# Emptying a convolution's PSUM on ScalarE instead of VectorE, with q placed between two pairs of spread attention weights

## The chip, the cores and the metric

The kernel runs on one core of one Trainium2 chip. A core has five engines that run their own instruction streams side by side: TensorE (PE: matmuls and transposes, its weight loads shown as PEld), VectorE (DVE), ScalarE (ACT), GpSimd (POOL) and SyncE (SP, which here only issues transfers). The metric is the device time in microseconds (us); it was 5517.69 us, the median of three runs (5511.05 to 5520.15).

## What is computed

Eight images of 256 channels and 64 x 64 pixels pass through two layers in fp32. Layer 0 adds a local attention over 3 x 3 neighbourhoods, with a second set of weights that a small generator makes from q, k and v. Layer 1 adds a deformable 3 x 3 convolution: for each pixel and each of nine taps an offset and a mask are computed, four neighbouring pixels are gathered, mixed, and multiplied with the convolution's weights.

```python
def _L0_conv_ref(x, ...):
    qkv = einsum('oc,bchw->bohw', w_qkv, x)              # q, k, v; 4 heads of 64 channels
    logits = einsum('bhdl,bhdkl->bhkl', q_flat, k_patch) # k: the 9 neighbours
    attn_out = einsum('bhkl,bhdkl->bhdl', softmax(logits, axis=2), v_patch)
    kernel = einsum('hkc,bhcl->bhkl', w_kg_g, cat) + b_kg
    conv_out = einsum('bhkl,bhdkl->bhdl', kernel, v_patch)
    return einsum('oc,bchw->bohw', w_proj, alpha * conv_out + beta * attn_out)

def _L1_conv_ref(x, w_off, b_off, w):                    # deformable convolution
    om = conv3x3(x, w_off) + b_off                       # 9 x (dy, dx), 9 masks
    v = the bilinear mix of the 4 pixels around each of the 9 moved taps, times sigmoid(mask)
    return einsum('bckhw,ock->bohw', v, w)

x = x + _L0_conv_ref(_gn(x), ...)                        # _gn: group norm, 32 groups
x = x + _L1_conv_ref(_gn(x), ...)                        # the x added here is called x1 below
```

## The kernel before

An image is cut into NC = 8 chunks of eight rows, N = 512 pixels. For layer 1 a chunk has KK = 9 taps, and a chunk with one tap is a slot: 72 slots an image, 576 in all. A slot's 512 pixels are NB = 4 blocks of 128, so there are 2304 blocks.

The main loop (the last lines of `preact_kernel`) walks the slots. In slot n, `transposes` turns the four summed blocks s on PE into PSUM (tile pt) and ACT copies them to SBUF (tile vt); `product(n - 1)` then multiplies the vt of the slot before with the weights into po, the two PSUM banks of pool `ps_o` in which the nine taps of a chunk add up: eight matmul instructions of 128 x 512, L848. `ahead(i)` works in advance for later slots and is called twice in each: two blocks' first corner is scaled by ACT (`scale`, L802), the other three corners of two earlier blocks are added by DVE (`sum_corners`, L810, six instructions), and POOL issues two gathers (`gather`, L786), each of 128 rows of 4 KB from the table in DRAM. Ten gathered blocks g have buffers, and ten sums s.

After nine taps a chunk ends. `finished` (L859) adds po and x1, which was read back from DRAM into r at the fifth tap, on DVE, and r is stored. Until both adds are done the next chunk's first `product` can't write po. In such a slot (the variable `last`) both calls of `ahead` stand before `product` and `finished`.

All else for the next image is cut into steps, a generator (`fronts`), of which about one runs in each slot, behind the product: 64 steps of attention (eight chunks of eight steps), some for the ends and norms, then `prepare`, which writes the next table and finds the offsets, one chunk a step. The first image's steps all run before the first slot, and beside the last image's slots there are none.

In attention, chunk c's steps also hold the second half of chunk c - 1 (d in the code). The first step of a chunk runs `d.spread_weights()`: four matmuls (tile wk, L492), each from 9 partitions of its own group of 32, spread the weights of a head over 100 keys, and DVE masks each from PSUM to SBUF (L500). Then `q` makes two tiles of q (psq, L293), which ACT copies (L301). The last chunk's weights are spread in a step of their own. All these results pass through `psum_a`, a pool of four PSUM banks used in turn: a new tile waits until the tile four before it has been read. Ahead of wk stand one bank for w and two for vk, which ACT copies.

`second_stats` stores each finished chunk of x1 to DRAM (`kept`, L565), from where `product` reads it back into r; `image`, the copy in SBUF, is overwritten by the next image during `prepare`. `to_table` (L648 to L657) turns a chunk, copies it into ts, one of four row buffers, and SP stores each twice in the table.

The order of instructions on PE, ACT, DVE and POOL is that of the program text (`tc.manual_schedule`); SP's order is left to the scheduler. Each engine works its own queue in order, so an instruction that waits holds up all behind it.

Of the kernel before, what the change touches and what calls it, by code (L numbers as in the profile page):

```python
# [9 lines left out]
F32 = mybir.dt.float32  # L10
# [7 lines left out]
P = 128  # L18
C = 256
NT = C // P  # L20
# [4 lines left out]
N = R * W  # L25
NB = N // P
NC = H // R
KK = 9
HEADS = 4
# [6 lines left out]
TP = R * WP // TJ  # L36
T = 8
KT = T + 2
# [8 lines left out]
SLOTS = NC * KK  # L47
# [10 lines left out]
def preact_kernel(ctx: ExitStack, tc: tile.TileContext, a: dict, out: bass.AP):  # L58
# [123 lines left out]
    p1 = ctx.enter_context(tc.tile_pool(name="p1", bufs=1))  # L182
    p2 = ctx.enter_context(tc.tile_pool(name="p2", bufs=2))

    wp = ctx.enter_context(tc.tile_pool(name="wp", bufs=NC + 3))
    ps_a = ctx.enter_context(tc.tile_pool(name="ps_a", bufs=4, space=PSUM))
    ps_t = ctx.enter_context(tc.tile_pool(name="ps_t", bufs=2, space=PSUM))
    ps_o = ctx.enter_context(tc.tile_pool(name="ps_o", bufs=1, space=PSUM))
# [90 lines left out]
    class Attention:  # L279
# [97 lines left out]
        def logits(self):  # L377

            G = self.G
            qk = self.qk.rearrange("p j c h (y x) -> p (j c h y) x", x=KT)  # L380
            by = p1.tile([P, G * KT, 3], F32, tag="by", name=f"by_{self.u}")
            nc.vector.tensor_reduce(
                by, qk[:, :, 0:9].rearrange("p g (a x) -> p g x a", x=3), AX.X, ALU.add
            )
            nc.vector.tensor_add(by[:, :, 0], by[:, :, 0], qk[:, :, 9])
            by = by.rearrange("p (g y) x -> p g (y x)", y=KT)
            self.lt = lt = p1.tile([P, G, KK], F32, tag="lt", name=f"lt_{self.u}")
            nc.vector.tensor_reduce(
                lt, by[:, :, 0:27].rearrange("p g (a k) -> p g k a", k=KK), AX.X, ALU.add
            )  # L390
            nc.vector.tensor_add(lt[:, :, 0:3], lt[:, :, 0:3], by[:, :, 27:30])
# [84 lines left out]
        def weights(self):  # L476
            ps = psum_a(f"w_{self.u}")
            for j in range(NB):
                nc.tensor.transpose(
                    ps[:, j * P : (j + 1) * P],  # L480
                    wts2[self.c % 2][:, j].rearrange("p h k -> p (h k)"),
                    ident,
                )
            self.wsb = p1.tile([P, N], F32, tag="wsb", name=f"wsb_{self.u}")
            nc.scalar.copy(self.wsb, ps)

        def spread_weights(self):

            self.wk = []
            for h in range(HEADS):  # L490
                ps = psum_a(f"wk_{self.u}_{h}")
                nc.tensor.matmul(  # L492
                    ps[:NK],
                    spread[32 * h : 32 * h + KK],
                    self.wsb[32 * h : 32 * h + KK],
                    start=True,
                    stop=True,
                )
                wk = p2.tile([NK, N], F32, tag="wk", name=f"wk_{self.u}_{h}", bufs=HEADS)
                nc.vector.tensor_mul(  # L500
                    wk.rearrange("p (t n) -> p t n", n=T * T),
                    ps[:NK].rearrange("p (t n) -> p t n", n=T * T),
                    near.unsqueeze(1).to_broadcast([NK, TC, T * T]),
                )
                self.wk.append(wk)
# [18 lines left out]
        def weighted(self, i):  # L524
            n = N // NH
            if i == 0:
                self.acc = p1.tile([P, NT, N], F32, tag="acc", name=f"acc_{self.u}")
            av = psum_a(f"av_{self.u}_{i}").rearrange("p (m n) -> p m n", m=NT)
            for g in range(2):
                for t in range(TC // NH):  # L530
                    for h in range(2):
                        o = 64 * (2 * g + h)
                        nc.tensor.matmul(  # L533
                            av[64 * h : 64 * h + 64, g, t * T * T : (t + 1) * T * T],
                            self.vk[:, t, o : o + 64],
                            self.wk[2 * g + h][:, i * n + t * T * T : i * n + (t + 1) * T * T],
                            start=True,
                            stop=True,
                        )
            nc.scalar.copy(self.acc[:, :, i * n : (i + 1) * n], av)  # L540
# [17 lines left out]
        def second_stats(self):  # L558
            for ct in range(NT):
                nc.vector.bn_stats(  # L560
                    self.stats[:, ct, self.c, :],
                    self.xt[:, ct, self.c * N : (self.c + 1) * N],
                )
            s = slice(self.c * N, (self.c + 1) * N)
            nc.sync.dma_start(kept[self.b % 2][:, :, s], self.xt[:, :, s])  # L565

    def attention(b):

        xt = image
        gn = norm0[b]  # L570
        gn.means()
        stats = p2.tile([P, NT, NC, 6], F32, tag="stats", name=f"stats1_{b}")
        yield None
        gn = gn.ready()
        xn = normed(xt, gn, 0)
        yield None
        d = None
        for c in range(NC):
            a_ = Attention(b, c, xn, stats)
            if d:  # L580
                d.spread_weights()
            a_.q(0)
            a_.q(1)
            yield None
            a_.k(0)
            a_.k(1)
            yield None
            a_.products()
            if d:
                d.weighted(0)  # L590
            yield None
            a_.logits()
            if d:
                d.keys(1)
                d.carry_v()
            a_.generated()
            a_.softmax_1()
            a_.carry_k()
            yield None
            a_.v(0)  # L600
            if d:
                d.weighted(1)
            a_.turned()
            a_.softmax_2()
            if c + 1 < NC:
                xn = normed(xt, gn, c + 1)
            yield None
            a_.v(1)
            if d:
                d.add(0, d.project(0))  # L610
            a_.softmax_3()
            yield None
            if d:
                d.add(1, d.project(1))
                d.second_stats()
            a_.weights()
            a_.keys(0)
            yield None
            d = a_
        d.spread_weights()  # L620
        yield None
        d.weighted(0)
        d.keys(1)
        yield None
        d.weighted(1)
        yield None
        for m in range(NT):
            d.add(m, d.project(m))
        d.second_stats()
        gn = Norm(stats, f"1_{b}")  # L630
        yield None
        gn.means()
        yield None
        yield gn.ready()

    def prepare(b, gn):
# [5 lines left out]
        def to_table(c, xn):  # L642
            for i in range(TJ // 2):
                ps = psum_a(f"ptab_{b}_{c}_{i}").rearrange("p (j e) -> p j e", j=2)
                for j in range(2):
                    o = WP + (2 * i + j) * TP
                    for ct in range(NT):
                        nc.tensor.transpose(  # L648
                            ps[:TP, j, ct * P : (ct + 1) * P],
                            xn[:, ct].rearrange("p r w -> p (r w)")[:, o : o + TP],  # L650
                            ident,
                        )
                ts = p2.tile([TP, 2, C], F32, tag="ts", name=f"ts_{b}_{c}_{i}", bufs=4)
                nc.scalar.copy(ts, ps[:TP])
                for q in range(2):
                    e = (R * c + 1 - q) * WP + 2 * i * TP
                    nc.sync.dma_start(  # L657
                        table[e : e + 2 * TP, q, :].rearrange("(j p) e -> p j e", p=TP), ts
                    )
# [151 lines left out]
                    s, g[:, q * C : (q + 1) * C], w[:, q : q + 1], s, ALU.mult, ALU.add  # L811
                )

    def ahead(i):

        scale(i + SCALE_AHEAD)
        scale(i + SCALE_AHEAD + 1)
        sum_corners(i + SUM_AHEAD)
        gather(i + LEAD)
        gather(i + LEAD + 1)  # L820
# [16 lines left out]
    def product(b, n):  # L837
        c, k = divmod(n, KK)
        if k == KK // 2:
            r = p1.tile([P, NT, N], F32, tag="r", name=f"r_{b}_{c}")  # L840
            nc.sync.dma_start(r, kept[b % 2][:, :, c * N : (c + 1) * N])
            state["r"] = r
        if k == 0:
            state["po"] = ps_o.tile([P, NT, 512], F32, tag="o", name=f"po_{b}_{c}")
# [9 lines left out]
                )  # L854

    def finished(b, c):
        po, r = state["po"], state["r"]
        for m in range(NT):
            nc.vector.tensor_add(r[:, m], po[:, m], r[:, m])  # L859
        nc.sync.dma_start(  # L860
            out[b].rearrange("(t p) l -> p t l", p=P)[:, :, c * N : (c + 1) * N], r
        )
# [7 lines left out]
    with tc.manual_schedule(engines=ordered):  # L870
# [20 lines left out]
        for n in range(B * SLOTS + 1):  # L891
# [3 lines left out]
            if n < B * SLOTS:  # L895
                transposes(*divmod(n, SLOTS))
                ahead(NB * n)
                if last:
                    ahead(NB * n + 2)
            if n > 0:  # L900
                product(*divmod(n - 1, SLOTS))
            if last:
# [3 lines left out]
            while (done - STEPS) * SLOTS < goal:  # L906
                next(steps, None)
                done += 1
            if n < B * SLOTS and not last:
                ahead(NB * n + 2)  # L910


def _constants():
# [75 lines left out]
```

## Time and profile before

The profile is of one execution of 5149.96 us, with a span of 5148.2 us from the first to the last instruction and a mean granted TensorE clock of 0.962.

| What | us | Where from |
|---|---|---|
| median of the timed runs | 5517.69 | three runs |
| profiled execution, span | 5149.96, 5148.2 | one execution |
| s sums on DVE, L810, 6912 | 2797.5 | 476 ns each |
| po matmuls, L848, 4608 | 2142.0 | 609 ns each, overlapping |
| vt copies on ACT, L834, 1152 | 611.5 | 583 ns each, from PSUM |
| psq matmuls, L293, 512 | 288.0 | 713 ns each, overlapping |
| wk masks on DVE, L500, 256 | 158.5 | 680 ns each |
| r adds on DVE, L859, 128 | 81.8 | 679 ns each |
| wk matmuls, L492, 512 | 80.6 | 635 ns each, overlapping |

The first image's steps take until 351.6 us; then eight images follow, the last of 423 us. In the profile's lines a name like "psq L293" is the tile written and the line; "A <- B" says that A's engine stood idle until B was done. A row of the view of waits gives the total in us, the number of waits and the longest. A row of the timeline gives start, length, engine, line, operation, tiles and count, and in brackets the idle time ahead of it and what ended it; neighbouring instructions of one kind are merged. Transfers kept the sixteen DMA engines busy 0.78 to 0.81 of the time in the first seven images; gathers are 1208 MB of the 1423 MB moved.

### The profile page before, as it was taken

How to read it: one execution, taken by the hardware profiler on the slowest of the kernel's cores; microseconds unless marked ns; L12 is line 12 of the kernel's file. 1: busy time of each engine (PE TensorE's matmuls, PEld its weight loads, DVE VectorE, ACT ScalarE, POOL GpSimd, SP SyncE). 2: the span in 40 equal slices, each digit the busy share in tenths (PEclk: the TensorE clock that was granted, in tenths of full speed). 3: DMA queues.
4: the chain of work that ended last, by engine and by line, in shares of the span. 5: the costliest groups of instructions: out<-in, count | busy, mean ns of one | idle time of the engine just before them, and what ended most of it. 6: DMA issues, size and time to landing. Idle time of an engine off the chain costs nothing. (4 is left out here: it accounts for less than half of the span.)

```text
span 5148.2 us, 79694 instructions
## 1 busy us (share of the span) xinstructions
PE 4726.1 (92%) x26592; PEld 2641.3 (51%) x26592; DVE 4206.1 (82%) x10128; ACT 2374.4 (46%) x5184; POOL 3193.9 (62%) x2310
## 2 busy tenths in 40 slices
PE   6979998999999999999999999999999999999888
PEld 4545554555545555455554555555554555554444
DVE  4568787878888888888888888888888888888888
ACT  2334444444444444454444444444444444444544
POOL 0027675666666666676665766756666566666776
PEclk9989999999999999999999999999999999999999
DMA  2067777887788777977779777888778877788998
GB/s 92 17 217 264 250 277 283 289 278 265 270 315 294 272 263 272 331 284 265 266 267 345 277 269 269 289 309 281 262 269 310 309 265 269 261 306 316 391 375 348
DMA packets 476841, 1422.61 MB, mean 276 GB/s; under 512 B 46910, under 2 KB 114750, under 8 KB 476300
## 3 DMA queue, kind: packets, MB, share of 16 engines
q0 software_dynamic: 331776, 1208.11, 66.1%
q1 hardware_dynamic: 141902, 204.27, 11.0%
q10 hardware_dynamic: 2750, 5.12, 0.3%
q8 instruction: 210, 3.44, 0.3%
q14 instruction: 203, 1.66, 0.1%
HBM read 1280.19 MB, written 137.13 MB: 275 GB/s over the span
## 5 line engine op out<-in xcount | busy, mean ns | idle before, releaser
L786 POOL DMA_INDIRECT g<-table,idx x2304 | 3191.4, 1385 | 1933.4 <-DVE s L810 513.4
L810 DVE SCALAR_TENSOR_TENSOR s<-g,wt,s 128x256 f32<-128x256 f32 x6912 | 2797.5, 476 | 401.3 <-ACT s L802 390.5
L848 PE MATMUL po<-vt,w_conv 128*128 128x512 f32 x4608 | 2142.0, 609 | 72.5 <-DVE r L859 72.5
L848 PEld LDWEIGHTS po<-vt,w_conv 128*128 128x128 f32 x4608 | 856.6, 196 | 947.0 <-issue 866.7
L802 ACT ACTIVATE s<-g,wt 128x256 f32<-128x256 f32 x2304 | 1081.8, 509 | 545.3 <-DMA g<-table,idx 473.3
L831 PE MATMUL pt<-ident,s 128*128 128x128 f32 x4608 | 693.5, 284 | 104.9 <-DVE s L810 73.0
L831 PEld LDWEIGHTS pt<-ident,s 128*128 128x128 f32 x4608 | 519.5, 143 | 401.9 <-DVE s L810 121.3
L834 ACT COPY vt<-pt 128x512 f32<-128x512 f32 x1152 | 611.5, 583 | 162.5 <-PE pt L831 161.7
L293 PE MATMUL psq<-xn,w_qkvT 128*128 128x512 f32 x512 | 288.0, 713 | 113.3 <-DVE wk L500 111.6
L301 ACT COPY q<-psq 128x512 f32<-128x512 f32 x128 | 75.0, 586 | 484.0 <-PE psq L293 484.0
L668 PE MATMUL om<-xn,w_off 128*32 128x512 f32 x2304 | 292.7, 605 | 0.0
L325 PE MATMUL psv<-xn,w_qkvT 128*128 128x264 f32 (+1 forms) x1088 | 263.9, 388 | 0.0
L293 PEld LDWEIGHTS psq<-xn,w_qkvT 128*128 128x128 f32 x512 | 111.4, 228 | 287.8 <-DVE wk L500 167.5
L371 DVE TENSOR_TENSOR qk<-qk,near_k 128x400 f32<-128x400 f32 x256 | 128.9, 565 | 158.6 <-PE qk L363 158.6
L325 PE MATMUL psk<-xn,w_qkvT 128*128 128x264 f32 (+1 forms) x1088 | 246.6, 381 | 2.1 <-ACT k L338 2.1
L325 PEld LDWEIGHTS psv<-xn,w_qkvT 128*128 128x128 f32 x1088 | 202.9, 193 | 84.5 <-issue 49.9
L545 PE MATMUL proj<-acc,w_projT 128*128 128x512 f32 x512 | 238.1, 592 | 0.7 <-ACT acc L540 0.7
L325 PEld LDWEIGHTS psk<-xn,w_qkvT 128*128 128x128 f32 x1088 | 202.2, 190 | 62.3 <-issue 18.9
L347 ACT COPY v<-psv 128x320 f32<-128x320 f32 (+1 forms) x272 | 110.1, 418 | 238.1 <-PE psv L325 238.0
L540 ACT COPY acc<-av 128x512 f32<-128x512 f32 x128 | 74.9, 585 | 265.1 <-PE av L533 264.7
L338 ACT COPY k<-psk 128x264 f32<-128x264 f32 (+1 forms) x272 | 100.6, 372 | 204.2 <-PE psk L325 204.0
L500 DVE TENSOR_TENSOR wk<-wk,near 100x512 f32<-100x512 f32 x256 | 158.5, 680 | 34.6 <-PE wk L492 34.6
(91 smaller groups left out, 3342.0 us busy)
## 6 DMA issues: line engine op xcount, KB each, us to landing
table<-ts SPq DMA_DIRECT2D x384, 176.0 KB
g<-table,idx POOLq DMA_INDIRECT x2304, 6.7
x<-in_x_dram SPq DMA_DIRECT2D x64, 512.0 KB
x<-x SPq DMA_DIRECT2D x64, 512.0 KB
r<-x SPq DMA_DIRECT2D x64, 512.0 KB
out_dram<-r SPq DMA_DIRECT2D x64, 512.0 KB
w_conv<-in_w_conv_dram ACTq DMA_DIRECT2D x1, 2304.0 KB
w_qkv<-in_w_qkv_dram ACTq DMA_DIRECT2D x2, 384.0 KB
```

What stands on the lines that cost most here:

```text
L293: nc.tensor.matmul(ps, w_qkvT[:, ct, m * P : (m + 1) * P], window(self.xn, ct, 4), start=(ct == 0), stop=(ct == NT - 1),)
L325: nc.tensor.matmul(ps[:, : (hi - lo) * WP], w_qkvT[:, ct, o : o + P], self.xn[:, ct, lo:hi, :], start=(ct == 0), stop=(ct == NT - 1),)
L371: nc.vector.tensor_mul(qk[:, 2 * jj : 2 * jj + 2, :, h, :], both[h][:, : 4 * NK].rearrange("p (j c k) -> p j c k", j=2, c=NT), near_k.unsq ...
L500: nc.vector.tensor_mul(wk.rearrange("p (t n) -> p t n", n=T * T), ps[:NK].rearrange("p (t n) -> p t n", n=T * T), near.unsqueeze(1).to_bro ...
L545: nc.tensor.matmul(ps, w_projT[:, ct, m * P : (m + 1) * P], self.acc[:, ct].rearrange("p (t y x) -> p y t x", y=T, x=T), start=(ct == 0), ...
L668: nc.tensor.matmul(ps[32 * g : 32 * g + 32, :], w_off[:, ct, k, :], window(xn, ct, k), start=(n < 4), stop=(n >= KK * NT - 4),)
L786: nc.gpsimd.indirect_dma_start(out=g, out_offset=None, in_=tables[b % 2], in_offset=bass.IndirectOffsetOnAxis(ap=found[b, c][0][:, j, k : ...
L802: nc.scalar.activation(s, g[:, 0:C], AF.Copy, scale=w[:, 0:1])
L810: nc.vector.scalar_tensor_tensor(s, g[:, q * C : (q + 1) * C], w[:, q : q + 1], s, ALU.mult, ALU.add)
L831: nc.tensor.transpose(pt[ct][:, j, :], s[:, ct * P : (ct + 1) * P], ident)
L834: nc.scalar.copy(v[:, ct, :], pt[ct].rearrange("p b n -> p (b n)"))
L848: nc.tensor.matmul(po[:, m, :], w_conv[:, ct, k, m * P : (m + 1) * P], v[:, ct, :], start=(k == 0 and ct == 0), stop=(k == KK - 1 and ct = ...
```

## The change

Six things are changed at once:

- `finished` no longer adds: ACT copies the two halves of po to a new tile y. A new function `stored` adds y and x1 on DVE in one instruction of 1024 elements and stores the sum; it stands at the end of the slot, behind the steps and the second `ahead`.
- In a slot that ends a chunk, only the two scales of the second `ahead` still stand ahead of `product`; its sums and gathers go behind the steps, where they stand in all other slots.
- `spread_weights` takes a pair of heads; q's two tiles are made between the first pair and the second. For the last chunk of an image both pairs follow each other as before.
- For the last image x1 is neither stored in `kept` nor read back; `stored` takes it from `image`.
- The table has six row buffers ts instead of four.
- The tile by shares a buffer with tw, wsb with gs, and acc with q; pool `wp` has ten buffers instead of eleven.

```diff
-    wp = ctx.enter_context(tc.tile_pool(name="wp", bufs=NC + 3))
+    wp = ctx.enter_context(tc.tile_pool(name="wp", bufs=NC + 2))
...
-            by = p1.tile([P, G * KT, 3], F32, tag="by", name=f"by_{self.u}")
+            by = p1.tile([P, G * KT, 3], F32, tag="tw", name=f"by_{self.u}")
...
-            self.wsb = p1.tile([P, N], F32, tag="wsb", name=f"wsb_{self.u}")
+            self.wsb = p1.tile([P, N], F32, tag="gs", name=f"wsb_{self.u}")
...
-        def spread_weights(self):
-
-            self.wk = []
-            for h in range(HEADS):
+        def spread_weights(self, i):
+
+            if i == 0:
+                self.wk = []
+            for h in (2 * i, 2 * i + 1):
...
-                self.acc = p1.tile([P, NT, N], F32, tag="acc", name=f"acc_{self.u}")
+                self.acc = p1.tile([P, NT, N], F32, tag="q", name=f"acc_{self.u}")
...
+
+            if self.b + 1 == B:
+                return
             s = slice(self.c * N, (self.c + 1) * N)
             nc.sync.dma_start(kept[self.b % 2][:, :, s], self.xt[:, :, s])
...
             if d:
-                d.spread_weights()
+                d.spread_weights(0)
             a_.q(0)
             a_.q(1)
+            if d:
+                d.spread_weights(1)
...
-                ts = p2.tile([TP, 2, C], F32, tag="ts", name=f"ts_{b}_{c}_{i}", bufs=4)
+                ts = p2.tile([TP, 2, C], F32, tag="ts", name=f"ts_{b}_{c}_{i}", bufs=6)
...
-    def ahead(i):
-
-        scale(i + SCALE_AHEAD)
-        scale(i + SCALE_AHEAD + 1)
+    def ahead(i, scaled=False):
+
+        if not scaled:
+            scale(i + SCALE_AHEAD)
+            scale(i + SCALE_AHEAD + 1)
         sum_corners(i + SUM_AHEAD)
         gather(i + LEAD)
         gather(i + LEAD + 1)
...
-            nc.sync.dma_start(r, kept[b % 2][:, :, c * N : (c + 1) * N])
+            if b + 1 < B:
+                nc.sync.dma_start(r, kept[b % 2][:, :, c * N : (c + 1) * N])
...
     def finished(b, c):
-        po, r = state["po"], state["r"]
+        po = state["po"]
+        y = p1.tile([P, NT, N], F32, tag="y", name=f"y_{b}_{c}")
         for m in range(NT):
-            nc.vector.tensor_add(r[:, m], po[:, m], r[:, m])
+            nc.scalar.copy(y[:, m], po[:, m])
+        state["y"] = y
+
+    def stored(b, c):
+        r, y = state["r"], state["y"]
+        x1 = r if b + 1 < B else image[:, :, c * N : (c + 1) * N]
+        nc.vector.tensor_add(r, y, x1)
         nc.sync.dma_start(
             out[b].rearrange("(t p) l -> p t l", p=P)[:, :, c * N : (c + 1) * N], r
         )
...
                 ahead(NB * n)
                 if last:
-                    ahead(NB * n + 2)
+                    scale(NB * n + 2 + SCALE_AHEAD)
+                    scale(NB * n + 3 + SCALE_AHEAD)
...
-            if n < B * SLOTS and not last:
-                ahead(NB * n + 2)
+            if n < B * SLOTS:
+                ahead(NB * n + 2, scaled=last)
+            if last:
+                stored(*last)
```

More of the change, by code (lines that the diff above doesn't have):

```diff
@@ L619, in attention @@
             d = a_
-        d.spread_weights()
+        d.spread_weights(0)
+        d.spread_weights(1)
         yield None
```

## The prediction

> **What bounds the kernel now.** I read the page's busy line first, then TensorE's waits, then the engines' time image by image, then two stretches of the timeline: one inside an image, one in the last.
>
> ```profile
> PE 4726.1 (92%) x26592; PEld 2641.3 (51%) x26592; DVE 4206.1 (82%) x10128; ACT 2374.4 (46%) x5184; POOL 3193.9 (62%) x2310
> ```
>
> TensorE (PE) is the engine with least spare time; VectorE (DVE) stands close behind. So the useful question is what PE waits for. The view of waits, PE alone, longest first:
>
> ```profile
> PE psq L293 <- DVE wk L500: 111.6, 49, 5.8
> PE pt L831 <- DVE s L810: 73.0, 144, 10.5
> PE po L848 <- DVE r L859: 72.5, 33, 7.3
> ```
>
> The first and third are what the change touches: 184 us of some 420 us of PE idleness. Busy time per image (columns: stretch, length, PE, PEld, DVE, ACT, POOL, clock, DMA share, GB/s), the fourth image and the last:
>
> ```profile
> 2239.50:2862.70 623.20, 581.85 (x3321) 328.10 (x3320) 523.65 (x1266) 294.19 (x648) 410.54 (x289) 0.97 0.80 284
> ...
> 4725.20:5148.20 423.00, 369.56 (x1161) 176.03 (x1159) 360.85 (x874) 207.29 (x429) 317.02 (x279) 0.93 0.95 371
> ```
>
> Images 0 to 6 are bound by PE with its waits (DMA 0.80 busy, DVE 84%); the last, with no attention beside it, by DMA (0.95). Now how the first wait arises, PE and then DVE:
>
> ```profile
> 2438.77 3.60 PE L848 MATMUL po<-vt,w_conv 128*128 128x512 f32 x8
> 2442.30 1.12 PE L492 MATMUL wk<-wsb,spread 9*100 9x512 f32 x8
> 2445.62 5.40 PE L293 MATMUL psq<-xn,w_qkvT 128*128 128x512 f32 x8 [2.21 <-DVE wk L500]
> ```
> ```profile
> 2440.15 4.82 DVE L810 SCALAR_TENSOR_TENSOR s<-g,wt,s 128x256 f32<-128x256 f32 x12
> 2444.89 2.47 DVE L500 TENSOR_TENSOR wk<-wk,near 100x512 f32<-100x512 f32 x4
> ```
>
> All four PSUM buffers hold wk; q needs the one that DVE empties first, and DVE is still in its sums until 2444.9. The reader should also see 5.40 us for eight q matmuls, where eight of the same shape in po took 3.60: the wait is followed by slow matmuls.
>
> [...]
> - [...] granted clock 0.80 over 2442.2 to 2450.9 and 0.72 over the same place a chunk earlier (2320.2 to 2332.4). A removed wait is thus worth more than its length.
> - [...] the eight wk instructions take 1.12 us, not the 3.60 of eight full ones. This is a price of splitting them.
> - [...] 601 ns for 432 elements (L445), 308 for 144 (L430), so 1.02 ns per element and about 160 fixed.
>
> **The change part by part.** The sum is against the profiled execution, 5149.96 us (span 5148.2). The median of the timed runs, 5517.69, is 7.1% longer, and no view shows why; I carry the result over as a ratio.
>
> *q between two pairs.* Order on PE is now wk0, wk1, q0, q1, wk2, wk3. The q's take PSUM buffers that ScalarE (ACT) emptied of vk a slot ago; the wait on DVE moves to wk2. Before, q could start 3.3 us after wk's start (1.12 + 2.21). Now PE reaches wk2 after one pair (about 1.05 us: two rounds, 0.51 apart in the trace, still needed for two row groups) plus 3.5 for the q's: 4.5 us. A DVE that comes at 3.3 is in time. The chunk with the longest wait, 5.8, has a finished tile's add and the second sums ahead of wk; these are moved behind the slot's steps (below), 1.28 + 2.45 = 3.7 us earlier, leaving about 2.1, also covered. So all 111.6 go. The slow clock: psq is busy 288.0 us in all; 64 chunks at 3.60 make 230.4; excess 57.6, which I count as gone with it. Gain 169.
> Price: PE runs a second pair as long as the quartet did, at 1.05 - 0.1 overlap = 0.95 us, in 56 chunks (the last chunk of each image issues all four together): 53. Bounds 0 (the extra falls into idle time) to 60 (1.12 - 0.05). I take 53, as the 3.5 us of q cover leaves PE no idle. Queued behind a late wk2 on PE are wk3 and then the next slot's transposes, for which ACT's vt waits: a miss would be felt at once.
>
> *ScalarE empties the convolution.* Removed from DVE: 128 adds of 679 ns from PSUM. Added: 128 ACT copies of 586 ns (row L834, same shape, from PSUM), 75 us on an engine 46% busy; one DVE add of 1024 elements, 160 + 1024 x 1.02 = 1.2 us, 64 times (77 against 87 us). In images 0 to 6 PE runs attention steps after the product, so 1.2 us of copies end before the next chunk's first product; 72.5 less the last image's 27.0 leaves 45.5, all gone. Of the slow clock in po (2142.0 less 576 x 3.60 = 68.4 excess), the last image's eight (6.64 for 3.60 and like it) make about 23, and the rest has several causes; I credit 15. Gain 60.
> In the last image the copies gain nothing:
>
> ```profile
> 4837.68 0.51 ACT L802 ACTIVATE s<-g,wt 128x256 f32<-128x256 f32 x1 [0.77 <-DMA g<-table,idx]
> 4838.96 0.51 ACT L802 ACTIVATE s<-g,wt 128x256 f32<-128x256 f32 x1 [0.77 <-DMA g<-table,idx]
> 4839.38 1.05 ACT L834 COPY vt<-pt 128x512 f32<-128x512 f32 x2
> ```
> ```profile
> 4840.27 6.64 PE L848 MATMUL po<-vt,w_conv 128*128 128x512 f32 x8 [3.32 <-DVE r L859]
> ```
>
> ACT is paced there by gathers, 1.28 us each; the two copies stand behind the fourth scale (ends 4839.47), so po would be free at about 4840.7, 0.4 later than now, and vt slips 1.1. Cost 8 x 0.4 = 3.
>
> *The moved sums.* In a slot that ends a chunk, two sums and their gathers go behind the steps, as they already do in the other eight. POOL's own order is unchanged. The transposes of the next slot need only sums issued in the first half, so nothing waits: 0, bounds -5 to +10.
>
> *Last x1 kept.* Eight loads and eight stores of 0.524 MB less. The stores lie under images with DMA 0.80 busy: 0. The loads are in the DMA-bound image: 4.19 MB at 371 to 411 GB/s, 10 to 11 us. Less the 3 above and 1 at the end (two copies and a 1.2 us add replace 1.36 of adds): 6.
>
> *Six table row buffers* end some of ACT's 49.0 us of waits for table<-ts, but PE is busy throughout in that stage (2732 to 2810: 78.00 of 78.00 us): 0, bounds 0 to 10. *Shared buffers* (by with tw, wsb with gs, acc with q, one idx buffer less): in each case the old reader stands before the new writer in the order already: 0.
>
> Sum: 169 - 53 + 60 + 6 = 182. What is late next: DVE, busy 524 of what would be about 597 us an image, 88%, with slots where it has no spare time (2347.3 to 2354.5: 7.1 of 7.2 us). I let it take back 12. Gain 170: 4980 us, ratio 0.967, so 5335 us in the timed runs.
>
> **The rivals.**
> - *DVE takes over* (20%). Of the 184 us of waits, all end on DVE. If it is simply the slower engine in those stretches, they return at pt<-s and qk. For: 82% on average and near full in five slots of nine. Against: after each psq wait it stands idle itself, because ACT, held by the late q, scales late (DVE s <- ACT s, 390.5 us in all). With half the gain of 229 lost and the pairs' 53 still paid: 229/2 - 53 + 6 = 68, so 5445 us.
> - *Slower by the split quartet* (13%). The place is wk on PE, the price 53 us (57 in timed runs). It decides once DVE is no longer late at q: then nothing is there to remove, and the price stays. DVE is late by only 2.2 us after five slots of about 37 us of PE work, so a PE some 6% slower than profiled would do, and the timed runs are 7.1% longer for a reason not shown. With po's part shrunk to 25 and 6 from the loads: 57 - 31 = +26, 5544 us.
> - *No visible change* (5%): in between, 5518.
> - The change fails to do what it says: the PSUM wait only moves from the adds to the copies in all images, not just the last; then 60 is lost, 182 - 60 = 122, 5387 us, inside the likeliest's range. Its chance is in the 62% of the forecast.
>
> **How the numbers follow.** Forecast 62%, own range 5260 to 5420: bounds of the clock credits (57.6 and 15 may be half) and of DVE's share below, all credited in full plus 25 from table buffers and last image above. The wide range 5255 to 5490 adds most of the DVE rival and leaves out the slower one: some 8 in 10. A measurement of this kernel tells 0.2%, 11 us, from no change. Faster 0.62 + 0.20 = 0.82, same 0.05, slower 0.13.
>
> **What would show it.** Right: psq <- wk nearly gone from PE's waits; psq busy near 230 us; wk's PE time up by some 50; po waiting only in the last image, now on ACT y; images 1 to 6 at about 597 us; DVE s <- ACT s well below 390. Wrong: a new wait of wk on DVE wk above 40 us, or pt <- s above 130, or images still over 615.

## The result, and the profile after

The change makes the kernel slower: 5727.98 us median against 5518.92, ratio 1.0371 (95% interval 1.0348 to 1.0394). 5335 was forecast.

These two medians come from a condition in which the kernel before takes 5474 to 5519 us (called B here), while the profile of the kernel before that the forecast read, and most experiments below, come from one in which the same kernel takes 5142 to 5150 us (called A); every comparison is made within one of them. The changed kernel's profiled run is of B (5734.62 us, span 5732.9). The only trace of the kernel before in B is of a run of 5463.6 us; none was taken where it needs 5519.

The busy line of the changed kernel's page:

```profile
PE 5045.4 (88%) x26592; PEld 2812.7 (49%) x26592; DVE 4209.9 (73%) x10064; ACT 2434.7 (42%) x5312; POOL 3440.9 (60%) x2310
```

DVE's busy time is what it was (4206), PE's has grown by 319 us with the same number of matmuls, and the idle time as well. PE's waits (us in total, times, longest):

```profile
PE qk L363 <- issue: 164.6, 276, 1.2
PE pt L839 <- DVE s L817: 111.6, 122, 10.9
PE pt L839 <- ACT vt L842: 105.7, 38, 10.2
PE av L534 <- issue: 89.8, 148, 1.1
...
PE po L857 <- ACT y L869: 29.9, 8, 8.9
```

The wait of psq on wk is gone, as forecast, and po waits for ACT's copies in eight places only (six of them in the last image). But the smallest matmuls, qk (the products) and av (the weighted values), now wait 254 us for "issue": for nothing that the profile shows. The fourth image and the last:

```profile
2454.80:3141.30 686.50, 625.45 (x3322) 350.42 (x3321) 524.31 (x1258) 302.37 (x664) 439.19 (x289) 0.93 0.74 258
5191.20:5732.90 541.70, 393.59 (x1160) 194.49 (x1160) 358.04 (x861) 211.13 (x447) 369.10 (x274) 0.84 0.74 276
```

686 us and 542 us, where 623 and 423 were before; DMA is less busy in both, 0.74 for 0.80 and 0.95. The q slot, PE, in that image:

```profile
2541.28 3.60 PE L857 MATMUL po<-vt,w_conv 128*128 128x512 f32 x8
2544.81 1.10 PE L493 MATMUL wk<-wsb,spread 9*100 9x512 f32 x4
2545.84 3.71 PE L293 MATMUL psq<-xn,w_qkvT 128*128 128x512 f32 x8
2549.49 1.10 PE L493 MATMUL wk<-wsb,spread 9*100 9x512 f32 x3
```

The place that the change was made for is as forecast: no wait, eight q matmuls in 3.71 us for 5.40, and a pair of wk as long (1.10) as the quartet was (1.12). The time is lost elsewhere. PE and then POOL (the gathers) in a products' slot of the same kernel:

```profile
2693.22 3.60 PE L857 MATMUL po<-vt,w_conv 128*128 128x512 f32 x8
2696.75 1.83 PE L363 MATMUL qk<-k,q 64*64 64x100 f32 x48
2698.90 0.24 PE L363 MATMUL qk<-k,q 64*64 64x100 f32 x1 [0.33 <-issue]
...
2702.47 0.39 PE L363 MATMUL qk<-k,q 64*64 64x100 f32 x4 [1.03 <-issue]
...
2705.34 1.97 PE L534 MATMUL av<-wk,vk 100*64 100x64 f32 x31 [0.55 <-issue]
```
```profile
2686.23 7.52 POOL L793 DMA_INDIRECT g<-table,idx  x1 [0.30 <-ACT vt L842]
2694.05 1.01 POOL L793 DMA_INDIRECT g<-table,idx  x1 [0.30 <-DVE s L817]
2695.37 0.94 POOL L793 DMA_INDIRECT g<-table,idx  x1 [0.30 <-ACT s L809]
2696.61 0.94 POOL L793 DMA_INDIRECT g<-table,idx  x1 [0.30 <-issue]
2697.86 0.94 POOL L793 DMA_INDIRECT g<-table,idx  x1 [0.30 <-issue]
...
2702.84 0.94 POOL L793 DMA_INDIRECT g<-table,idx  x1 [0.30 <-issue]
```

After 48 of the 64 products PE starts one to four matmuls at a time, while POOL issues a gather every 1.24 us without a pause. In A the same kernel has the same slot, with nearly the same gathers (7.51, 1.01, 0.94, 0.93, 0.94 ...), and PE does this in it:

```profile
2417.17 3.60 PE L857 MATMUL po<-vt,w_conv 128*128 128x512 f32 x8
2420.70 1.63 PE L363 MATMUL qk<-k,q 64*64 64x100 f32 x64
2422.31 1.15 PE L534 MATMUL av<-wk,vk 100*64 100x64 f32 x32
2423.39 1.09 PE L839 MATMUL pt<-ident,s 128*128 128x128 f32 x8
```

2.8 us for both groups there, 10.6 in B. So two questions were put to the chip: what the change is worth by its parts, and which part of it meets B's condition so badly. Sums of qk and av below run from the start of a slot's first product to the end of the last av matmul behind it, waits included, over the 56 such slots that gathers run beside; a "run" of gathers is a row of them that start less than 1.32 us apart.

### The profile page after: what moved, and what is told of

The parts are those of the page before. It is cut to its first block, busy times and chain, and to the rows that moved or that the text cites. A ratio compares the mean times of both kernels' runs of the same rounds, so it can differ in the third digit from the quotient of the medians.

```text
span 5732.9 us, 79673 instructions
## 1 busy us (share of the span) xinstructions
PE 5045.4 (88%) x26592; PEld 2812.7 (49%) x26592; DVE 4209.9 (73%) x10064; ACT 2434.7 (42%) x5312; POOL 3440.9 (60%) x2310
## 5 line engine op out<-in xcount | busy, mean ns | idle before, releaser
L793 POOL DMA_INDIRECT g<-table,idx x2304 | 3438.3, 1492 | 2268.7 <-DVE s L817 778.3
L857 PE MATMUL po<-vt,w_conv 128*128 128x512 f32 x4608 | 2205.8, 624 | 53.8 <-ACT y L869 29.9
L857 PEld LDWEIGHTS po<-vt,w_conv 128*128 128x128 f32 x4608 | 889.8, 204 | 966.0 <-issue 933.8
L839 PE MATMUL pt<-ident,s 128*128 128x128 f32 x4608 | 754.1, 303 | 263.2 <-DVE s L817 111.6
L839 PEld LDWEIGHTS pt<-ident,s 128*128 128x128 f32 x4608 | 563.7, 153 | 573.6 <-DVE s L817 151.7
L363 PE MATMUL qk<-k,q 64*64 64x100 f32 x4096 | 214.2, 263 | 167.8 <-issue 164.6
L534 PE MATMUL av<-wk,vk 100*64 100x64 f32 x4096 | 223.0, 258 | 91.7 <-issue 89.8
L363 PEld LDWEIGHTS qk<-k,q 64*64 64x64 f32 x4096 | 138.0, 136 | 266.0 <-issue 260.5
L534 PEld LDWEIGHTS av<-wk,vk 100*64 100x64 f32 x4096 | 185.2, 166 | 159.7 <-issue 129.8
L293 PE MATMUL psq<-xn,w_qkvT 128*128 128x512 f32 x512 | 249.4, 631 | 1.6 <-DVE xn L242 1.6
```

Of the source, the lines that this page charges most:

```text
L293: nc.tensor.matmul(ps, w_qkvT[:, ct, m * P : (m + 1) * P], window(self.xn, ct, 4), start=(ct == 0), stop=(ct == NT - 1),)
L363: nc.tensor.matmul(both[h][64 * t : 64 * t + 64, n : n + NK], self.qt[r, ct, o * T * T : (o + 1) * T * T], kt[r, ct, :, T * o : T * o + KT ...
L534: nc.tensor.matmul(av[64 * h : 64 * h + 64, g, t * T * T : (t + 1) * T * T], self.vk[:, t, o : o + 64], self.wk[2 * g + h][:, i * n + t * ...
L793: nc.gpsimd.indirect_dma_start(out=g, out_offset=None, in_=tables[b % 2], in_offset=bass.IndirectOffsetOnAxis(ap=found[b, c][0][:, j, k : ...
L839: nc.tensor.transpose(pt[ct][:, j, :], s[:, ct * P : (ct + 1) * P], ident)
L857: nc.tensor.matmul(po[:, m, :], w_conv[:, ct, k, m * P : (m + 1) * P], v[:, ct, :], start=(k == 0 and ct == 0), stop=(k == KK - 1 and ct = ...
```

## The experiments

**The parts in A.** First the kernel before, unchanged, then q between the pairs alone, then all but that.

> The kernel before, unchanged, for a profile beside those of the changed kernel. The profile on record spans 5148 us, while the timed runs take 5518. Theory A (PE's small matmuls of qk and av starve in any kernel of this form, and the profile on record was an exception): span about 5515, with PE qk <- issue and av <- issue waits of 100 us or more in total, as in the changed kernel (158 and 85 us). Theory B (the change itself creates these waits): the longer span comes from elsewhere, and qk <- issue stays below 20 us.

5145.5 us, ratio 0.9999 (0.9987 to 1.0012). Its trace has the lines of the forecast's profile (psq on wk 112.0 us, po on r 70.7) and no wait for issue in qk. That profile was thus sound, but for A.

```diff
             if d:
-                d.spread_weights()
+                d.spread_weights(0)
             a_.q(0)
             a_.q(1)
+            if d:
+                d.spread_weights(1)
```

> The kernel before with q between two pairs of spread weights, nothing else. Theory A (the wait at q was what let the small matmuls behind it be issued in time; without it PE comes to qk and av too early and starves): slower than before by 150 us or more, qk and av <- issue above 200 us in total, psq <- wk near 0. Theory B (the moved sums and gathers and ScalarE's copies do the harm, and the split is a gain as forecast): faster than before by 60 to 130 us.

5105.7 us, ratio 0.9925 (0.990 to 0.995): 40 us won, no waits for issue. In this condition neither theory's number was met: the version is not slower, and the gain is under 60. The same version again, in a later comparison:

> The kernel before with q between the two pairs alone, once more, for the case that the comparison is of the kind in which the kernel before takes 5475 to 5519 us. Theory G' (q between the pairs makes the runs of gathers without a pause long, and long runs starve the engines there): at 5146 us this kernel has 386 gathers that are the fourth or a later one of such a run in the images 0 to 6, the changed kernel 375, the kernel before 185, the change without q 161; so it has the waits for issue at qk and av, over 100 us, and a ratio over 1.00, about 1.03. Theory B' (the moved sums, the scales ahead and the ScalarE copies lose it): few waits for issue, ratio 0.98 to 0.995. Where the kernel before takes 5145: 5106 again, within 8.

5096.4 us, ratio 0.9919 (0.9891 to 0.9947), again A, so it told nothing of B. All but the pairs (the changed kernel with `d.spread_weights(0)` and `(1)` both ahead of q):

> The changed kernel with all four spread weights ahead of q again; all other parts stay changed. Theory A: the loss is the split's, so this is within 40 us of before or faster (5450 to 5560), and psq <- wk is back at 60 us or more. Theory B: the loss stays, 5680 us or more, with the last image near 540 us as in the changed kernel.

5152.9 us, ratio 1.0012 (1.0001 to 1.0023). Theory A's line (within 40 us of before) is met, but it decides nothing here: condition A shows the loss in neither half. Two more things are seen: the other images gain some 2 us each, and the last image takes 451.1 us for 416.4. (The kernel before itself took 416.4, 423.0 and 423.1 us for the last image in its three traces of A, so differences of up to 7 us there say nothing.)

> The changed kernel itself, beside the runs in which the kernel before takes about 5146 us. Theory C: the loss of 209 us belongs to the condition in which the two kernels were compared (there the kernel before takes 5519), and here the parts add up: -40 from q between the pairs (alone 5105.7 against 5145.9) and +7 from all the rest (5152.9), so 5113 us, within 15; no waits for issue in the products' and weighted slots. Theory D: the parts act on each other, which neither part alone could show: the waits for issue return (over 200 us of PE idle in qk, av), the ratio is over 1.02 here too, 5250 us or more.

The changed kernel in A: 5073.4 us against 5143.5, ratio 0.9871 (0.9841 to 0.9900), so it is faster there, by more than its parts alone (40 and -7). Theory C's kind of answer, though 40 us below its number; theory D is out. Its fourth image and its last:

```profile
2206.60:2810.80 604.20, 582.66 (x3322) 326.19 (x3321) 523.73 (x1257) 302.63 (x663) 423.26 (x289) 0.98 0.82 293
4622.20:5070.80 448.60, 370.35 (x1161) 179.95 (x1159) 358.85 (x865) 215.84 (x447) 338.67 (x280) 0.91 0.88 341
```

**The order of q and wk.** The kernel before with q first and the quartet whole:

```diff
-            if d:
-                d.spread_weights()
             a_.q(0)
             a_.q(1)
+            if d:
+                d.spread_weights()
```

> The kernel before with q's two halves issued ahead of the whole quartet of spread weights, so that q waits for no bank and the quartet stays one burst. If splitting the quartet is what costs the pairs of the change about 1.1 us a chunk, this keeps q's gain without that price: 5050 us or so (ratio 0.98), with PE's warm time per image back at that of the kernel before. Rival: the quartet now waits behind q for its banks and k behind the quartet, the wait only moves from q to k: 5145 (ratio 1.00), with a new wait psk <- DVE wk of about 100 us.

5075.1 us, ratio 0.9879 (0.9848 to 0.9910): better than the pairs by 31 us, in two comparisons whose intervals just touch. 18 of these lie in the first steps (347.1 us against 365.4), where PE has 54.7 us at the slow clock with the pairs and 18.0 here. What makes the clock fall with the pairs was not shown.

**The moved sums, and the last image.** The changed kernel with the sums from PSUM on DVE and the old order (`nc.vector.tensor_add(r[:, m], po[:, m], x1[:, m])` in `finished`, both `ahead` calls as before):

> The changed kernel with the convolution's PSUM emptied by VectorE's sums straight from PSUM, in the order of the kernel before; all else of the change stays. If the moved emptying is what loses 35 us in the last image, this is the best so far: e3 less 35 less or more the po wait of the other images, ratio 0.985 or so (5070). If the buffers, the sharing or the kept x1 lose them, it stays within 10 us of the changed kernel.

5089.5 us, ratio 0.9904 (0.9872 to 0.9936). By the medians the ScalarE emptying is worth 16 us in all, which the overlapping intervals do not make certain. In the traces 37 are won in images 0 to 6 (4292 us against 4255) and 32 lost in the last (416.4 against 448.6); another 8 lie in the first steps, where nothing was changed. The same undone in the last image alone:

> The changed kernel with the emptying, the sum and the order of the kernel before in the last image alone. If the last image's 35 us come from the ScalarE emptying there, they return: 35 us below the changed kernel, with a last image of about 416; if not, the last image stays near 451.

5048.4 us, ratio 0.9817 (0.9781 to 0.9853), last image 428.4: 25 us came back by the medians, 20 of the image's 32 in the traces. The moved emptying alone, with x1 read from DRAM in the last image too and four row buffers:

```diff
-        po, r = state["po"], state["r"]
+        po = state["po"]
+        y = p1.tile([P, NT, N], F32, tag="y", name=f"y_{b}_{c}")
         for m in range(NT):
-            nc.vector.tensor_add(r[:, m], po[:, m], r[:, m])
+            nc.scalar.copy(y[:, m], po[:, m])
...
+    def stored(b, c):
+        nc.vector.tensor_add(r, y, r)
```

> The kernel before with the emptying by ScalarE and the moved sums alone (and the shared buffers that make room for them); x1 of the last image comes from DRAM again, four row buffers, the spread weights ahead of q. Where the kernel before takes 5145: the change without q took 5153, and lost 35 us in the last image and won 2 us in each other image; if that loss is all of the moved emptying, this takes 5153 to 5165, with a last image near 451 to 461; if the kept x1 or the row buffers had a share in it, 5130 or less. Where it takes 5475: theory G' (q between the pairs makes the long runs of gathers): no long runs here (about 160 late gathers), few waits for issue, ratio 1.00 to 1.01; theory B' (the moved sums and the scales ahead lose it there): ratio 1.02 or more, waits for issue over 100 us.

5141.0 us, ratio 0.9990 (0.9979 to 1.0000), last image 425.5. So the copies alone cost 2 to 9 us there, hardly more than that image varies by, and some 26 more come only with the kept x1 and the six row buffers (451.1), which were not tried apart; x1 kept and six row buffers with DVE's sums (416.4, above) cost nothing. Why they do it together is open. What is seen is the gathers: in the changed kernel the last image's DMA share falls from 0.96 to 0.88, and behind seven of the nine tiles that are finished in it two gathers start 7.5 to 9.5 us apart. With the kernel before there are six such places, of 5.5 to 6.7 us.

**Toward a version that beats both in A.** First both corrections together:

> A version meant to beat both kernels: the change, with the quartet of spread weights undivided behind q's two halves, and the last image emptied and summed as in the kernel before. Theory: the two corrections add up, because they work in different stages: the undivided quartet was worth 31 us against the pairs (5075.1 against 5105.7, in two comparisons), the last image 25 us (5048.4 against 5073.4). So 5020 us within 15, ratio 0.976, where the kernel before takes about 5145. Rival: the undivided quartet's 31 us were mostly the first steps and the waits that the ScalarE emptying has removed anyway; then it stays at 5048 within 8. If this comparison is of the kind in which the kernel before takes about 5519, the theory that the stalls in the products' slots come from the order q between the pairs gives a ratio below 1.00, and the theory that they come from gathers without pause beside the small matmuls leaves the ratio at 1.02 or more.

5063.7 us, ratio 0.9844 (0.9826 to 0.9861): by the median worse than the version with the last image alone as before (5048.4), and neither theory's number. The first steps gained 23 us, but images 0 to 5 lost about 6 each. A part of that is wk, which now waits for ScalarE to empty q (16.9 us in all). Hence the quartet whole in image 0 alone:

```diff
-            if d:
+            if d and b:
                 d.spread_weights(0)
             a_.q(0)
             a_.q(1)
+            if d and not b:
+                d.spread_weights(0)
             if d:
                 d.spread_weights(1)
```

> e6 (the change with the last image emptied and summed as in the kernel before) with the quartet undivided behind q in image 0 alone, whose attention mostly runs in the first steps, and the pairs from image 1 on. Theory: the pairs cost 20 us in the first steps (369.9 us against 347.2, cold clock 62 us against 18) and nothing in the images, so 20 us below e6: 5028 us within 10, ratio 0.977, first steps near 347. Rival: the later first image makes up for it (the kernel is paced there by the table rows), and it stays at 5048 within 8.

5041.7 us, ratio 0.9803 (0.9787 to 0.9820), the lowest in A, though not clear of the 0.9817 above: the number is the rival's (5048 within 8). The first steps take 344.7 us as the theory said, but images 0 to 6 gave 14 of the 25 us back.

**What B is made of.** The changed kernel with pauses between the gathers:

```diff
         rows[i] = g
+        if i % 2:
+            for _ in range(6):
+                nc.gpsimd.memset(pause, 0.0)
```

> The changed kernel with six small memsets on GpSimd after every second gather, so that gathers stand in runs of two at most. Theory G (the loss of the recorded comparison comes from long runs of gathers without a pause, in which the other engines start few instructions: VectorE 1.5 starts per us beside the first two gathers of a run, 0.65 beside the fourth, 0.32 beside the sixth, where the same kernel at 5073 us has 1.7, 1.7 and 2.3): in a comparison where the kernel before takes about 5519 the ratio falls from 1.037 to 1.00 or below; where the kernel before takes about 5145 there is no such starving to remove, and the pauses cost nothing to 30 us: 5073 to 5105. Rival (the runs are an effect of the stalls, not their cause): the ratio stays at 1.03 there; where the kernel before takes 5145 it says the same as theory G. Rival 2 (GpSimd is short of time and pauses push the last image, which the gathers pace, by 288 gathers x 0.5 us = 140 us): over 5150 us.

This comparison had B: 5849.8 us against 5475.4, ratio 1.0676 (1.0648 to 1.0703). The waits for issue went (PE gaps over 0.3 us at qk and av: 243 us to 20), qk and av took 283 us for 586 (64 of the 283 are waits of av for VectorE), and the time rose all the same. PE's waits show why:

```profile
PE po L861 <- ACT y L873: 293.7, 48, 9.8
PE pt L843 <- DVE s L821: 144.9, 168, 9.3
PE pt L843 <- ACT vt L846: 80.5, 116, 5.8
```

ScalarE waited 1777 us for gathers: a pair with its pause takes at least 4.0 us, 576 of an image's 690. So the pauses remove the stall and put a pace in its place. Theory G holds for the stall, but its ratio of 1.00 or below was missed, and the time is as rival 2 has it (over 5150): this gave no remedy. A lighter pause (`if i % 3 == 2`, three memsets), together with the kernel before for its trace:

> The kernel before, unchanged, for its trace where it takes about 5480 us. Theory G (runs of gathers without a pause starve the other engines, and the change makes more and longer runs: 194 of four or more against 132 at 5073 and 5150 us): the kernel before has the same stalls there, but fewer of them: waits for issue at the small matmuls of 60 to 150 us against the changed kernel's 243, VectorE's starts beside the fourth gather of a run under 1.0 per us. Theory P (all of its stages are longer by the same share, a slower chip): instructions of every kind longer by 7%, no waits for issue. Where it takes 5145, it is as before: no waits for issue, and says nothing on either.

> The changed kernel with a pause of three memsets on GpSimd (about 0.8 us) after every third gather alone; the six memsets after every second gather left qk's and av's waits for issue at 20 us of 243, but took 4.0 us for each pair of gathers, close to all the time that an image has for them. Theory G: where the kernel before takes about 5480, the waits for issue stay under 60 us, and the gathers keep up (1.5 us each): ratio below 1.00. Rival (the stalls only take another form, and whatever makes this condition slow holds back every gather's consumers): ratio 1.03 or more again. Where the kernel before takes 5145: 5075 to 5110, ratio 0.987 to 0.993.

Both fell in A: 5148.4 us, and 5295.5 with ratio 1.0301 (1.0272 to 1.0329). Against the changed kernel's 0.9871 the light pauses cost 0.043, some 220 us for the 2 to 37 expected, with ScalarE's waits for gathers at 1167 us. What the lighter pause does in B was not seen.

Then B came again, for four kernels. The change without the pairs:

> The change without q between the pairs (all four spread weights ahead of q), for the case that the comparison has the recorded condition (kernel before 5475 to 5519). Theory G': no long runs of gathers (161 late ones against 375 of the changed kernel), so the waits for issue at qk and av stay under 100 us and the ratio at 1.01 or less. Theory B': the moved sums and the scales ahead lose it, ratio 1.02 or more. Where the kernel before takes 5145: 5153 again, within 8.

5479.7 us against 5476.2, ratio 0.9986 (0.9963 to 1.0009). In B this clears the moved sums, the kept x1 and the buffers of the loss (its waits for issue, 98.0 us, stay just under theory G's 100).

> q between the two pairs alone, in the recorded condition if the comparison has it again (the change without q took 5480 against 5476 there, ratio 0.9986, so the moved sums are cleared). Theory G': q alone brings the loss: ratio 1.02 to 1.04 and waits for issue at qk and av of over 150 us. Theory I (interaction: only q and the moved sums together lose it): ratio 0.99 to 1.01. Where the kernel before takes 5145: 5100 again.

q between the pairs alone: 5695.6 us (two runs) against 5473.9, ratio 1.0402 (1.0371 to 1.0432), the whole loss. Theory G' holds, theory I is out. PE's waits, largest first and av's:

```profile
PE qk L363 <- issue: 190.0, 294, 1.8
...
PE av L534 <- issue: 41.8, 72, 1.2
```

The kernel before:

> The kernel before, for its trace in the recorded condition. Theory G': waits for issue at the small matmuls, as in the changed kernel but of less than half the sum (under 120 us against 243), and late gathers of runs without a pause about half of the changed kernel's. Theory P (every stage slower alike): none.

5463.6 us (one run). Its PE waits:

```profile
PE pt L831 <- ACT vt L834: 130.4, 39, 9.9
PE psq L293 <- DVE wk L500: 109.3, 46, 5.8
PE qk L363 <- issue: 76.1, 143, 1.8
```

It has the stall too, but little of it. A products' slot, POOL and then PE:

```profile
2425.88 0.94 POOL L786 DMA_INDIRECT g<-table,idx  x1 [0.30 <-issue]
2430.26 0.94 POOL L786 DMA_INDIRECT g<-table,idx  x1 [3.45 <-ACT s L802]
2431.51 0.94 POOL L786 DMA_INDIRECT g<-table,idx  x1 [0.31 <-issue]
2437.83 2.84 POOL L786 DMA_INDIRECT g<-table,idx  x1 [5.38 <-ACT s L802]
```
```profile
2430.75 1.34 PE L363 MATMUL qk<-k,q 64*64 64x100 f32 x49
2432.30 0.41 PE L363 MATMUL qk<-k,q 64*64 64x100 f32 x5 [0.20 <-issue]
2433.02 0.50 PE L363 MATMUL qk<-k,q 64*64 64x100 f32 x10 [0.31 <-issue]
2433.73 1.15 PE L533 MATMUL av<-wk,vk 100*64 100x64 f32 x32 [0.21 <-DVE qk L371]
```

The late q had moved the products into a pause of the gathers: two of them stand beside the products, with gaps of 3.45 and 5.38 us around. With q on time they meet a run of eight. Set side by side (the run that the products stand in, median; qk and av, 56 slots):

| kernel | A: run | A: qk and av | B: run | B: qk and av |
|---|---|---|---|---|
| before | 2 | 156.5 us | 2 | 307.4 us |
| all but the pairs | 2 | 147.0 us | 2 | 335.1 us |
| q between the pairs alone | 7 | 167.2 us | 8 | 558.7 us |
| the change | 7 | 147.0 us | 8 | 586.4 us |
| the change, paused | - | - | 2 | 283.4 us |

In A the length of the run costs nothing: 147.0 us with runs of 2 and of 7. (Of the 156.5 and 167.2 us, 9 and 19 are waits of av for VectorE, which leaves 147 and 148.) In B the time goes with the run, inside one kernel too: in the trace of the kernel before, PE waits for issue 0.8 us on average in the 43 slots whose run has at most three gathers, and 5.8 us in the four whose run has six or more. From before to q between the pairs, qk and av grow by 251 us (558.7 less 307.4) and the spans by 234 (5695.7 less 5461.7); from before to the change it is 279 and 271. The control lies in the first steps, before any gather: the same sum over the eight slots there is 22.5 us in every trace, A or B.

> The best version (pairs from image 1 on, the last image emptied as in the kernel before; 0.980 where the kernel before takes 5143) in the recorded condition, if the comparison has it. Theory G': it has q between the pairs, so it loses there too: ratio 1.02 or more. Rival (the last image alone, 542 us in the changed kernel, made the loss): 1.00 or less. Where the kernel before takes 5145: 5042 again, within 10.

5673.1 us (two runs), ratio 1.0361 (1.0331 to 1.0391), qk and av 551 us: the version that is lowest in A loses in B as the change does. Of the four versions measured in both conditions, none is better than the kernel before in both. The others were measured in one condition only, q first with the whole quartet among them.

## Why the prediction was wrong

The step that failed is the carry: "The median of the timed runs, 5517.69, is 7.1% longer, and no view shows why; I carry the result over as a ratio." The 7.1% were not spread over the kernel. From its trace in A to that in B (5141.8 and 5461.7 us) the kernel before gets 320 us longer: 151 at qk and av beside gathers (307.4 less 156.5), 118 in the last image (534.4 less 416.4), the rest in other slots, and nothing in the first steps (354.5 and 350.2 us), which have no gathers. The change moves work into just such places, so it cannot scale: 0.987 in A becomes 1.037 in B. Two traces lay a condition apart, and the forecast had a number for that gap (7.1%), but no bound for what the change would do within it.

By the prediction's own steps:

- *q between two pairs.* "All 111.6 go": right, in A and B. "Excess 57.6, which I count as gone with it": psq fell from 290.9 to 248.4 in A, 42 for 58. "Price 53": wk's PE time rose from 80.5 to 142.9, 62. These make 92 for 116, of which the version with the pairs alone saw 40: PE's idle time fell by 77 us and not 112 (other waits took over, av on qk, wk on q and po on r with 27 of it), and pt and po ran 19 us longer; 11 us were lost in the first steps, where PE has 54.7 us at the slow clock for 17.3 in the trace that the forecast read. The slow clock is thus partly moved, not won.
- *The slow clock.* The prediction reads "A removed wait is thus worth more than its length" from a place where q waited 2.21 us and the granted clock was 0.80. The trace has the clock at half for 3.41 us from 2446.65 us on, 4.35 us after wk began there and 1.03 us after q's wait had ended; q matmuls then take up to 1061 ns, the last of the eight 592. With the wait gone the eight take 3.71 us (above) for 5.40, but what makes the clock fall was not shown.
- *Queued behind.* "Queued behind a late wk2 on PE are wk3 and then the next slot's transposes": the work asked about was too near. What counted was two slots on, and on another engine: which gathers would be beside the products once PE is early.
- *ScalarE empties the convolution.* "Gain 60": 37 in images 0 to 6. "All gone" is too much there: po still waits 38 us outside the last image (66.7 less 28.5), of 53 with DVE's sums. "Cost 8 x 0.4 = 3" in the last image: 32. The forecast priced the copies as a delay of PE; what is seen instead are gathers that start late and a lower DMA share.
- *Last x1 kept.* "6": not seen with DVE's sums (416.4 and 416.4, but the 7 us by which that image varies would hide it), a loss together with ScalarE's copies.
- *Six row buffers, shared buffers*: not tried alone.
- *DVE takes 12 back*: about twice that; pt's wait on s is 97.2 us in A for 73.0, and now the longest. But it does not come from a PE that is early: with q between the pairs alone it is 71.0, with all but the pairs 91.1.

In A the sum was 170 us and 70 were measured: right in sign, with the last image and what came in the place of q's wait as the wrong terms. In B the sign was wrong. The rival "slower by the split quartet" came near in time (5544, measured 5728) but not in cause: its price is real in B too (wk's PE time 80.7 to 143.5 us), but so was the wait that it said would be gone (109.3 us in the kernel before).

The signs told little. Most of those for "right" came true in B while the time grew: psq's wait gone, wk's PE time up by 59 us, DVE's wait for ACT's scales at 229 us. Of those for "wrong", wk did not wait on DVE and pt on s stayed at 112; only "images still over 615" spoke.

## What to carry to other kernels

Where the timed runs are some per cent slower than the profiled one, the profile does not show what the timed runs lose; a forecast for them needs a trace from there, or a bound for how the change meets the unknown loss, and not a ratio. When a wait is removed, ask not only what is queued behind it but what other engines will be doing at the place where the freed engine then arrives: here a wait that looked useless had kept bursts of 96 small matmuls out of a run of gathers, which in B was worth more than the wait (251 us at qk and av against 109.3). And in a stage that transfers pace, an instruction put on the engine that frees their buffers can cost more than its own length: the last image's 16 copies of 0.59 us, some 9 us, went with up to 35 us there. So count the transfers that start late, and try the parts apart.

## What the runs showed of the hardware

- In B VectorE starts fewer instructions beside an unbroken run of gathers. Its starts per us in the changed kernel, between one gather's start and the next, from the first to the sixth gather of a run: 1.49, 1.50, 0.93, 0.65, 0.55, 0.32; in A the same kernel has 1.71, 1.59, 1.83, 1.74, 1.81, 2.29. The gathers go on at 1.24 us each, and their 4 KB packets take a median of 159 ns in both.
- It is not the fetching of instructions, as far as the DMA records show: the 16 KB fetches take 975 ns in B and 977 in A (medians), and in some stalled slots (at 1322 us, where the products take 7.8 us) none lies between the first and last product.
- The traces of B lack event records. They hold 50,494 to 51,231 semaphore updates and some 33,500 DMA landings, those of A about 65,500 and 45,700; the paused kernel in B lies between (65,193 and 40,599). The lack is greatest where the stalls are: in the changed kernel 5969 DMA completions in the products' slots left 2888 landing records and 4553 in the last image 1914, while between the first gather and the end some 33,500 others left 27,000. So B shows waits and missing records together; whether the recording of the runs is what makes B was not shown. No run without records was made, so what B is stays open. It does not go with the chip's number: on chip 10 the kernel before took 5143.5 us in one comparison (A) and 5476.2 in another (B).
- A memset of 128x64 on GpSimd takes 156 ns on average. Three of them take 0.59 us from the first start to the last end, and after every third gather, 768 times, they made the kernel some 220 us longer in A though GpSimd was idle a third of the time. So the idle time of GpSimd did not hide them: a third to a half of their sum came out as time, with ScalarE waiting for gathers.
